# Load stage in program order, 33 early steps with a 128-column state, and two pieces of work moved ahead

## The chip, the cores and the metric

One core of one Trainium2 chip. The metric is device time in microseconds (us), the median of several runs; one more execution is taken by the hardware profiler. Engines: TensorE (PE; its weight loads are shown apart as PEld), VectorE (DVE), ScalarE (ACT), GpSimd (POOL) and SyncE (SP), which only issues DMAs here.

## The reference

Two layers on x of shape 16 x 128 x 64 x 64 (batch, channel, row, column), float32, each with a residual:

```python
x = x + _L0_conv_ref(_gn(x), ...)     # group norm, then a diagonal LSTM
x = x + _L1_conv_ref(_gn(x), ...)     # group norm, then a 4-qubit circuit per pixel
```

The diagonal LSTM skews the image (row i is shifted right by i, zeros are filled in) and scans over the columns of the skewed image:

```python
def step(carry, ist):
    h, c = carry
    h_shift = jnp.pad(h, ((0, 0), (0, 0), (1, 0)))[:, :, :-1]     # state of the row above
    s_s = einsum(w_ss[:, :, 0], h_shift) + einsum(w_ss[:, :, 1], h) + b_ss
    gates = ist + s_s                                             # ist: w_is @ x + b_is
    o, f, ig = split(sigmoid(gates[:, :3 * C])); g = tanh(gates[:, 3 * C:])
    c_new = f * c + ig * g
    h_new = o * tanh(c_new)
    return (h_new, c_new), h_new
```

A row that has not begun (its columns are still the filled zeros) also has a state. It depends neither on the image nor on the batch, only on how many steps have gone by: a chain of 64 vectors of 128 channels, the same for all waiting rows. The second layer projects 128 channels to four angles, needs sines of them, two matmuls with a square between, and adds the result.

## The kernel before

The 16 images stay in on-chip memory as a ring of 40 of the 64 rows (`ring`, L107); the other 24 pass through later. There are three stages.

**Load.** `rows(b)` (L361) loads 40 rows of image b into the ring in two DMAs of 1 MB and 256 KB on SP. The loop at L372 then loads the other 24 rows in three pieces of 256 KB (`rest`, a pool of 4 buffers), takes `bn_stats` of all eight pieces of 512 elements (L381) and `bn_aggr` (L382), always image by image: ring pieces first, then the rest pieces of the same image. These statistics give the first group norm; nothing of the scan can start without them: `group_mean` (L134), four VectorE operations, `group_rstd` (L140), then `normalised(0)` (L464) and `gate_ps(0)` (L485).

Beside that run the weights: eleven small DMAs on ACT's queue, twelve transposes in pairs of PSUM banks (L241 to L247), the circuit's coefficients on VectorE and ACT (L257 to L276), and the chain of waiting rows. `inv_step(j)` (L174) makes vector j+1 from vector j: four matmuls with the weights `wsT` and one moving column (L184), four activations (L194), three POOL products (L198 to L200), tanh (L202) and a scaling (L204), which gives `hinv[j+1]`, the input of the next. `EARLY` = 27 of them are spread over the images of the load. The load stage is ordered by the planner, not by hand.

**Scan.** 160 steps (`step`, L571), from L694 on in program order. At step t up to 32 row slots are active, in two bands; each step has the state products (L582), the gates' activations (L608), the cell update, and the input products of the next step (L491). A narrow step (`plain`, at most 96 columns) multiplies the state by w1T and w0T directly; a wide one takes wsT first and then differences. While fewer than 32 slots are active one waiting row advances with the step (`waits`, L548), from vector `EARLY` on. In steps 32 to 37 the last vectors are made by `inv_step` inside the step (L578 and the `next(inv, None)` lines), for L677 to read later. Four or six `bn_stats` of finished rows per step (`statistics`, L535) prepare the second group norm: group g is four rows of all 16 images, and group 9 of 16 ends with step 135.

**Join and quantum layer.** After the last step the statistics that are left (20 pieces), then over all 32 half-pieces of each image (L703 to L715): sum, group mean, deviations, squares, sum, `group_rstd`; then `w_image` (L721) and the images of the second layer, bound by DMA and TensorE in turn.

Queues are in program order per engine: a waiting instruction holds all behind it on its engine. DMAs on SP wait for a free buffer in the same way.

Of the kernel before, what the change touches and what calls it, by code (L numbers as in the profile page):

```python
# [11 lines left out]
F32 = mybir.dt.float32  # L12
# [15 lines left out]
EARLY = 27  # L28
# [50 lines left out]
def kernel(  # L79
# [60 lines left out]
    def group_rstd(pool, psum, var, rstd, which, scale):  # L140
        ps = psum.tile([P, NB], F32, name=f"gv{which}", tag="small")
        nc.tensor.matmul(ps, lhsT=group, rhs=var, start=True, stop=True)
        nc.vector.tensor_scalar(var, ps, scale, EPS, ALU.mult, ALU.add)
        sd = pool.tile([P, NB], F32, name=f"sd{which}", tag="gn_sd")
        nc.scalar.activation(sd, var, AF.Sqrt)
        r0 = pool.tile([P, NB], F32, name=f"r0{which}", tag="gn_r0")
        nc.vector.reciprocal(r0, sd)

        nc.vector.tensor_mul(sd, r0, r0)
        nc.vector.tensor_mul(sd, sd, var)  # L150
        nc.vector.tensor_scalar(sd, sd, -0.5, 1.5, ALU.mult, ALU.add)
        nc.vector.tensor_mul(rstd, r0, sd)  # L152

    small = ctx.enter_context(tc.tile_pool(name="small", bufs=2))
    with ExitStack() as scan:
# [13 lines left out]
        for v in (*hst, *xns, none):  # L169
            nc.gpsimd.memset(v, 0.0)  # L170
# [3 lines left out]
        def inv_step(j, pool=None):  # L174


            one = ps_small.tile([P, 4], F32, name=f"inv_ps{j}", tag="small") if pool is None else None
            ps = {}
            for g in ORDER:
                if pool is None:  # L180
                    ps[g] = one[:, g : g + 1]
                else:
                    ps[g] = pool.tile([P, 1], F32, name=f"inv_ps{j}_{g}", tag=f"inv{g}")
                nc.tensor.matmul(  # L184
                    ps[g],
                    lhsT=wsT[:, g * 128 : (g + 1) * 128],
                    rhs=hinv[:, j : j + 1],
                    start=True,
                    stop=True,
                )  # L190
            yield
            ac = small.tile([P, 4], F32, name=f"inv_a{j}", tag="inv_a")
            for g in ORDER:
                nc.scalar.activation(ac[:, g : g + 1], ps[g], FUNC[g], bias=bias[:, g : g + 1])  # L194
            yield
# [7 lines left out]
            yield  # L203
# [3 lines left out]

        with ExitStack() as prep:
            pp = prep.enter_context(tc.tile_pool(name="prep", bufs=1))
            rest_pool = prep.enter_context(tc.tile_pool(name="rest", bufs=4))  # L210
            ps_prep = prep.enter_context(tc.tile_pool(name="ps_prep", bufs=2, space=PSUM))
            ps_inv = prep.enter_context(tc.tile_pool(name="ps_inv", bufs=1, space=PSUM))


            wx_n = pp.tile([P, 4, P], F32, name="wx_n")
            ws_n = pp.tile([P, 4, 2 * P], F32, name="ws_n")
            nc.scalar.dma_start(out=wx_n, in_=w_is.rearrange("(g o) c -> o g c", o=P))
            nc.scalar.dma_start(out=ws_n, in_=w_ss.rearrange("(g o) c k -> o g (c k)", o=P))
            b_n = pp.tile([8, P], F32, name="b_n", tag="rows")
            nc.scalar.dma_start(out=b_n[0:4], in_=b_is.rearrange("(g o) -> g o", o=P))  # L220
            nc.scalar.dma_start(out=b_n[4:8], in_=b_ss.rearrange("(g o) -> g o", o=P))
            nc.scalar.dma_start(out=wide_sb, in_=wide)
            four_sb = pp.tile([4, 272], F32, name="four_sb")
            nc.scalar.dma_start(out=four_sb, in_=four)
            qw = pp.tile([P, 24], F32, name="qw")
# [3 lines left out]
            prew = pp.tile([4, P], F32, name="prew")  # L229
            preb = pp.tile([4, 1], F32, name="preb")  # L230
            post_n = pp.tile([P, 4], F32, name="post_n")
            nc.scalar.dma_start(out=prew, in_=pre_w)
            nc.scalar.dma_start(out=preb, in_=pre_b.rearrange("(w one) -> w one", one=1))
            nc.scalar.dma_start(out=post_n, in_=post_w)
            nc.scalar.dma_start(out=b_out, in_=post_b.rearrange("(o one) -> o one", one=1))

            ident = pp.tile([P, P], F32, name="ident")
            make_identity(nc, ident)


            for g in range(4):  # L241
                for n, (dst, src) in enumerate(
                    ((wxT, wx_n[:, g, :]), (w0T, ws_n[:, g, 0::2]), (w1T, ws_n[:, g, 1::2]))
                ):
                    tp = ps_prep.tile([P, P], F32, name=f"tp{g}_{n}", tag="tp")
                    nc.tensor.transpose(tp, src, ident)
                    nc.scalar.copy(dst[:, g * 128 : (g + 1) * 128], tp)  # L247
            nc.vector.tensor_add(wsT, w0T, w1T)
            tp = ps_prep.tile([P, 8], F32, name="bias_ps", tag="tp")
            nc.tensor.transpose(tp, b_n, ident[0:8, 0:8])  # L250
            nc.scalar.copy(bias, tp[:, 0:4])
            nc.vector.tensor_add(bias, bias, tp[:, 4:8])
            nc.vector.memset(hinv[:, 0:1], 0.0)
            nc.vector.memset(cinv[:, 0:1], 0.0)
# [4 lines left out]
            nc.vector.tensor_add(ang[:, 1, 0, :], q3[:, 0, :], q3[:, 2, :])  # L259
            nc.vector.tensor_sub(ang[:, 1, 1, :], q3[:, 0, :], q3[:, 2, :])  # L260
            nc.vector.tensor_copy(ang[:, 1, 2, :], q3[:, 1, :])
            nc.vector.tensor_scalar(
                ang[:, 0], ang[:, 1], 1.0 / (4.0 * math.pi), 0.25, ALU.mult, ALU.add
            )
            nc.vector.tensor_scalar_mul(ang[:, 1], ang[:, 1], 1.0 / (4.0 * math.pi))
            rnd = pp.tile([P, 2, 3, 8], F32, name="rnd")
            nc.vector.tensor_scalar(rnd, ang, ROUND, ROUND, ALU.add, ALU.subtract)
            nc.vector.tensor_sub(ang, ang, rnd)
            trig = pp.tile([P, 2, 3, 8], F32, name="trig")
            nc.scalar.activation(trig, ang, AF.Sin, scale=TWO_PI)  # L270
            co = gates.tile([P, 8, 8], F32, name="co")
            nc.vector.tensor_mul(co[:, 0], trig[:, 0, 0, :], trig[:, 0, 2, :])
            nc.vector.tensor_mul(co[:, 1], trig[:, 1, 0, :], trig[:, 0, 2, :])
            nc.vector.tensor_mul(co[:, 2], trig[:, 0, 1, :], trig[:, 1, 2, :])
            nc.vector.tensor_mul(co[:, 3], trig[:, 1, 1, :], trig[:, 1, 2, :])
            nc.vector.tensor_scalar_mul(co[:, 4:8], co[:, 0:4], -1.0)  # L276


            tp = ps_prep.tile([P, 16], F32, name="wt_ps", tag="tp")
            nc.tensor.matmul(tp, lhsT=prew, rhs=four_sb[:, 0:16], start=True, stop=True)  # L280
            nc.gpsimd.memset(w_image, 0.0)
            for j in range(8):
                nc.scalar.copy(w_theta[:, 16 * j : 16 * j + 16], tp)
            tp = ps_prep.tile([P, 1], F32, name="bt_ps", tag="tp")
            nc.tensor.matmul(tp, lhsT=four_sb[:, 16:144], rhs=preb, start=True, stop=True)
# [605 lines left out]
```

## Time and profile before

| | |
|---|---|
| median of 3 runs | 1467.23 us (1466.18 to 1468.28) |
| profiled execution, its time | 1469.78 us |
| its span | 1468.0 us |
| mean granted TensorE clock | 0.984 |
| busy: PE, PEld, DVE, ACT, POOL | 1363.1, 968.9, 975.8, 767.7, 889.9 us |
| HBM read, written | 59.61 MB, 46.14 MB |
| load: first TensorE product of the scan starts at | 110.73 us |
| scan: last statistics of the last step begin at | 1298.87 us |
| quantum layer: first angles at | 1314.52 us |

The span runs from the first to the last instruction; the execution's own time has some 2 us around it. Busy times of TensorE are of pipelined instructions and their ends are modelled, so a busy TensorE need not be one at its peak. A float32 product shows as two instructions. Idle time of an engine costs nothing where the engine isn't the one waited for.

### The profile page before, as it was taken

The numbers are of one execution on the slowest core, as the hardware profiler recorded it, in microseconds if no ns is written. First come the engines' busy times: TensorE is split into PE (matmuls) and PEld (weight loads), VectorE is DVE, ScalarE is ACT, GpSimd is POOL, SyncE is SP. The second block draws the span as 40 slices with busy tenths as digits, with TensorE's granted clock in tenths as the row PEclk, the third lists the DMA queues.
The fourth block names the chain that finished last, engine by engine and source line by source line (L and its number), as shares of the span: only waits on it lengthen the run. The fifth ranks groups of instructions, "written<-read, shape, count | busy, mean of one in ns | idle before, by whom it ended". The sixth has DMA issues, their size and how long they took to land. (4 is left out here: it accounts for less than half of the span.)

```text
span 1468.0 us, 19391 instructions
## 1 busy us (share of the span) xinstructions
PE 1363.1 (93%) x5798; PEld 968.9 (66%) x5798; DVE 975.8 (66%) x2458; ACT 767.7 (52%) x1862; POOL 889.9 (61%) x1694
## 2 busy tenths in 40 slices
PE   4658999999999999999999999999999999858987
PEld 3648887777776677667766776677677787842322
DVE  6883566566666666887777675555555687767775
ACT  3544666565555555555555555555555565533231
POOL 1115777766776677778887776677667676521110
PEclk9999999999999999999999999999999999979996
DMA  9980000000000000133344000000000000028996
GB/s 306 359 277 1 1 2 0 1 1 1 1 0 1 1 0 1 58 115 116 127 138 137 2 1 0 1 1 1 1 1 1 1 1 2 1 86 288 316 333 236
DMA packets 86192, 106.99 MB, mean 73 GB/s; under 512 B 4024, under 2 KB 70728, under 8 KB 86088
## 3 DMA queue, kind: packets, MB, share of 16 engines
q1 hardware_dynamic: 80576, 92.29, 18.6%
q0 software_dynamic: 3840, 12.59, 2.5%
q10 hardware_dynamic: 1672, 0.89, 0.2%
q8 instruction: 46, 0.75, 0.2%
q14 instruction: 58, 0.48, 0.1%
HBM read 59.61 MB, written 46.14 MB: 72 GB/s over the span
## 5 line engine op out<-in xcount | busy, mean ns | idle before, releaser
L491 PE MATMUL ps<-xn,wxT 128*128 128x512 f32 (+18 forms) x1280 | 480.7, 518 | 2.0 <-POOL xn L483 2.0
L604 DVE TENSOR_TENSOR ps<-ps,both 128x256 f32<-128x256 f32 (+9 forms) x544 | 219.7, 408 | 325.6 <-PE ps L582 320.0
L608 ACT ACTIVATE ps<-ps,bias 128x512 f32<-128x512 f32 (+23 forms) x480 | 268.4, 581 | 253.0 <-DVE ps L604 213.1
L491 PEld LDWEIGHTS ps<-xn,wxT 128*128 128x128 f32 x1280 | 231.8, 191 | 174.5 <-issue 155.5
L633 ACT COPY both<-ps 128x256 f32<-128x256 f32 (+9 forms) x544 | 191.5, 355 | 178.6 <-PE ps L582 158.9
L582 PE MATMUL ps<-diff,w1T 128*128 128x256 f32 (+14 forms) x1088 | 283.7, 363 | 0.0
L582 PE MATMUL ps<-diff,w0T 128*128 128x256 f32 (+14 forms) x1088 | 283.2, 362 | 0.0
L524 POOL TENSOR_TENSOR ring<-ring,hst 128x256 f32<-128x256 f32 (+8 forms) x488 | 247.2, 538 | 24.7 <-DVE hst L672 24.7
L582 PEld LDWEIGHTS ps<-hst,wsT 128*128 128x128 f32 x1088 | 195.9, 190 | 85.5 <-DVE hst L672 35.4
L582 PE MATMUL ps<-hst,wsT 128*128 128x256 f32 (+14 forms) x1088 | 241.3, 365 | 5.7 <-DVE hst L672 4.2
L582 PEld LDWEIGHTS ps<-diff,w0T 128*128 128x128 f32 x1088 | 199.7, 190 | 21.2
L582 PEld LDWEIGHTS ps<-diff,w1T 128*128 128x128 f32 x1088 | 199.2, 190 | 20.9
L483 POOL TENSOR_TENSOR xn<-xn,rstd 128x512 f32<-128x512 f32 (+10 forms) x160 | 170.7, 1067 | 15.2 <-DVE rstd L152 2.7
L478 POOL TENSOR_TENSOR xn<-ring 128x256 f32<-128x256 f32 (+8 forms) x213 | 147.1, 700 | 0.0
L672 DVE TENSOR_TENSOR hst<-g,ps 128x256 f32<-128x256 f32 (+13 forms) x320 | 108.5, 369 | 45.0 <-ACT g L663 41.7
L663 ACT ACTIVATE g<-cst 128x256 f32<-128x256 f32 (+20 forms) x320 | 103.0, 368 | 63.8 <-DVE cst L662 63.3
L473 POOL TENSOR_TENSOR xn<-ring,mean 128x16 f32<-128x16 f32 (+8 forms) x247 | 130.5, 537 | 7.0 <-DVE mean L138 6.0
L515 POOL TENSOR_TENSOR diff<-hst 128x240 f32<-128x240 f32 (+9 forms) x136 | 103.2, 759 | 39.0 <-DVE hst L672 35.6
L662 DVE TENSOR_TENSOR cst<-cst,ps 128x256 f32<-128x256 f32 (+20 forms) x320 | 104.6, 368 | 5.5
L659 DVE TENSOR_TENSOR ps<-ps,g 128x512 f32<-128x512 f32 (+20 forms) x160 | 95.2, 595 | 19.1 <-ACT g L608 17.8
L685 POOL COPY edge<-hst 128x16 f32<-128x16 f32 x64 | 25.1, 392 | 136.0 <-DVE hst L672 136.0
L652 DVE TENSOR_TENSOR cst<-cst,ps 128x512 f32<-128x512 f32 (+20 forms) x160 | 92.8, 580 | 16.9 <-ACT ps L608 9.4
(152 smaller groups left out, 1217.6 us busy)
## 6 DMA issues: line engine op xcount, KB each, us to landing
ring<-in_x_dram SPq DMA_DIRECT2D x16, 1024.0 KB, 7.6
out_dram<-ring SPq DMA_DIRECT2D x16, 1024.0 KB, 5.7
rest<-in_x_dram SPq DMA_DIRECT2D x48, 256.0 KB, 5.2
low<-ring SPq DMA_DIRECT2D x6, 2048.0 KB, 7.5
ring<-in_x_dram SPq DMA_DIRECT2D x6, 2048.0 KB, 8.1
low<-low POOLq DMA_DIRECT2D x48, 256.0 KB, 5.2
out_dram<-low SPq DMA_DIRECT2D x48, 256.0 KB, 5.1
ring<-in_x_dram SPq DMA_DIRECT2D x16, 256.0 KB, 7.9
```

Source lines behind the costliest of these rows:

```text
L473: nc.gpsimd.tensor_sub(by_pairs(xn, 0, j, n), x0, over(mean1, n))
L478: nc.gpsimd.tensor_sub(by_pairs(xn, 1, j, n), lower, of)
L483: nc.gpsimd.tensor_mul(v, v, r)
L491: nc.tensor.matmul(ps[g][:, :, a:b], lhsT=wxT[:, g * 128 : (g + 1) * 128], rhs=xns[t % 2][:, :, a:b], start=True, stop=True,)
L515: nc.gpsimd.tensor_sub(diff[:, 0, a1:b], now[:, 1, a1 - NB : b - NB], now[:, 0, a1:b])
L524: nc.gpsimd.tensor_add(x1, x1, by_pairs(new, q, j, n))
L582: nc.tensor.matmul(out, lhsT=w[:, g * 128 : (g + 1) * 128], rhs=rhs, start=False, stop=True, skip_group_check=True,)
L604: nc.vector.tensor_add(v, v, both[g][:, a:b])
L608: nc.scalar.activation(to[:, :, a:w], ps[g][:, :, a:w], FUNC[g], bias=bias[:, g : g + 1])
L633: nc.scalar.copy(both[g][:, a:b], ps[g][:, 0, a:b])
L662: nc.vector.tensor_add(c[:, q], c[:, q], ig[:, q])
L672: nc.vector.tensor_mul(new[:, q, a:v], th[:, q, a:v], act[GO][:, q, a:v])
```

## The change

Load stage: it is put into program order by hand. SP's order becomes `rows(b+2)`, then the rest pieces of image b+1 (`behind`); VectorE takes the ring pieces of image b+1 before the rest pieces of image b. `rest` has 7 buffers, four of which hold weights at first. The first image comes in five pieces. Six of the small loads go from ACT's queue to POOL's, `w_ss` comes first and its two taps are added before the transposes; four transposes share one PSUM bank and one copy. The circuit's coefficients are made on POOL. The other weights' transposes stand between the first five waiting-row steps.

Waiting rows: 33 steps in place of 27 are made in the load and none in the scan. The moving operand is the state vector read 128 times (a broadcast), and each step is followed by two matmuls whose result nobody reads (`keep`).

Hand-over: the state products of step 0 are issued before the statistics' last part; the input products add to them. Three more `keep` products stand before the first group mean and one after the variance's matmul.

Second statistics: once group 9 is done (`FIRST` = 10 groups), `early_sums` makes their mean, deviations, squares and sums, one operation per scan step, ahead of that step's `statistics`. At the end only six groups are left, taken about that mean, and one matmul turns both sums into group values. `inverse_root` has one operation fewer than `group_rstd`.

```diff
-EARLY = 27
+EARLY = 33
+FIRST = 10
...
-    def group_rstd(pool, psum, var, rstd, which, scale):
-        ps = psum.tile([P, NB], F32, name=f"gv{which}", tag="small")
-        nc.tensor.matmul(ps, lhsT=group, rhs=var, start=True, stop=True)
-        nc.vector.tensor_scalar(var, ps, scale, EPS, ALU.mult, ALU.add)
...
+    def inverse_root(pool, var, rstd, which):
+
         r0 = pool.tile([P, NB], F32, name=f"r0{which}", tag="gn_r0")
...
+        nc.scalar.activation(sq, var, AF.Sqrt)
+        nc.vector.reciprocal(r0, sq)
+        nc.vector.tensor_mul(sq, r0, r0)
+        nc.vector.scalar_tensor_tensor(sq, sq, -0.5, var, ALU.mult, ALU.mult)
+        nc.vector.scalar_tensor_tensor(rstd, sq, 1.5, r0, ALU.add, ALU.mult)
...
+        def inv_step(j, pool):
+
+
             ps = {}
+            rhs = hinv[:, j : j + 1].to_broadcast([P, P])
             for g in ORDER:
...
+                ps[g] = pool.tile([P, P], F32, name=f"inv_ps{j}_{g}", tag=f"inv{g}")
+                w = wsT[:, g * 128 : (g + 1) * 128]
+                nc.tensor.matmul(ps[g], lhsT=w, rhs=rhs, start=True, stop=True)
...
-            rest_pool = prep.enter_context(tc.tile_pool(name="rest", bufs=4))
...
+            rest_pool = prep.enter_context(tc.tile_pool(name="rest", bufs=7))
...
+            prep.enter_context(tc.manual_schedule())
+
+            ws_n = [rest_pool.tile([P, 2, 2 * P], F32, name=f"ws_n{i}", tag="rest") for i in range(2)]
+            sum_n = rest_pool.tile([P, 4, P], F32, name="sum_n", tag="rest")
+            wx_n = rest_pool.tile([P, 4, P], F32, name="wx_n", tag="rest")
...
+            def keep(pool, tag, v):
+
+                ps = pool.tile([P, v.shape[-1]], F32, name=nc.get_next_instruction_name(), tag=tag)
+                nc.tensor.matmul(ps, lhsT=ident, rhs=v, start=True, stop=True)
 
             rows(0)
             rows(1)
+            behind(0)
+            turned()
+            for k in (1, 2):
+                statistics(0, k)
...
+            transposed("wsT", wsT, lambda g: sum_n[:, g, :])
+            biases()
+            coefficients()
...
             for b in range(NB):
                 if b + 2 < NB:
                     rows(b + 2)
...
+                if b + 1 < NB:
+                    behind(b + 1)
+                    for k in (1, 2, 3, 4, 0):
+                        statistics(b + 1, k)
+                for k in (5, 6, 7):
+                    statistics(b, k)
+                aggregated(b)
                 while b < NB - 1 and done * (NB - 1) < EARLY * (b + 1):
-                    for _ in inv_step(done, ps_inv):
-                        pass
+                    inv_step(done, ps_inv)
+                    keep(ps_keep, "keep", ring[:, 2, b, 0:P])
+                    keep(ps_keep, "keep", wsT[:, 0:P])
+                    if between:
+                        between.pop(0)()
                     done += 1
...
+            first = {}
+            for g in ORDER:
+                first[g] = ps_gate.tile([P, 2, NC], F32, name=f"ps0_{g}", tag="gate")
+                for w, rhs in ((w1T, hst[0][:, :, 0 : LEAST // 2]), (w0T, above(hst[0], 0, LEAST // 2))):
+                    nc.tensor.matmul(
...
+            for v in (ring[:, 2, NB - 1, :], rests[NB - 1][0], rests[NB - 1][1]):
+                keep(ps_small, "small", v)
+
             group_mean(ps_small, mv1[:, :, 0], mean1, 1, 1.0)
...
+            nc.tensor.matmul(ps, lhsT=group, rhs=var, start=True, stop=True)
+            keep(ps_gate, "gate", wxT)
+            nc.vector.tensor_scalar_add(var, ps, EPS)
+            inverse_root(pp, var, rstd1, 1)
...
+        def early_sums():
+            k = 2 * FIRST
+            total(moments[:, 0], 0, k)
+            yield
+            group_mean(ps_small, moments[:, 0], mean2, 2, 1.0 / k)
+            less_mean(0, k)
+            yield
+            total(moments[:, 0], 0, k)
+            yield
+            yield from squared(0, k)
+            total(moments[:, 1], 0, k)
...
-        j = t + EARLY - 2
-        inv = inv_step(j) if SLOTS <= t and j < NH - 1 else iter(())
...
+            for later in sums:
+                next(later, None)
             statistics(4 if w - a <= LEAST else 6)
...
+            k, n = 2 * FIRST, 2 * NG2
+            less_mean(k, n)
+            total(more[:, 0], k, n)
+            for _ in squared(k, n):
+                pass
+            total(more[:, 1], k, n)
+            nc.vector.tensor_add(moments, moments, more)
+            ps = ps_small.tile([P, 2, NB], F32, name="gm3", tag="small")
+            nc.tensor.matmul(ps, lhsT=group, rhs=moments, start=True, stop=True)
+            nc.vector.tensor_scalar_mul(moments, ps, 1.0 / n)
+            var = small.tile([P, NB], F32, name="var2", tag="gn_var")
+            nc.vector.tensor_mul(var, moments[:, 0], moments[:, 0])
+            nc.vector.tensor_sub(var, moments[:, 1], var)
+            nc.vector.tensor_scalar_add(var, var, EPS)
+            inverse_root(small, var, rstd2, 2)
+            nc.vector.tensor_add(mean2, mean2, moments[:, 0])
```

## The prediction

> **What bounds the kernel now.** I read the page's slices first, then busy time by stretches of a few us, then the timeline of each stretch that the diff touches, and the chain of waits at the end.
>
> ```profile
> PE   4658999999999999999999999999999999858987
> DMA  9980000000000000133344000000000000028996
> ```
>
> Each digit is 36.7 us. There are three stages: the load (to 106 us, DMA near full, TensorE half idle), the scan (TensorE full to 1299 us), and the quantum layer. The diff touches the load, the hand-over to the scan, six scan steps, a few late steps and the join at 1299 to 1313 us.
>
> In the load, by stretches (busy us of PE, PEld, DVE, ACT, POOL, then granted clock, DMA share, GB/s):
>
> ```profile
> 40.00:50.00 10.00, 6.47 (x28) 6.21 (x29) 8.56 (x16) 5.24 (x21) 1.72 (x9) 1.00 1.07 372
> ...
> 96.00:98.00 2.00, 1.29 (x7) 1.21 (x6) 1.45 (x3) 1.27 (x6) 0.58 (x3) 1.00 0.45 161
> 98.00:100.00 2.00, 1.68 (x8) 1.68 (x8) 1.52 (x3) 0.99 (x4) 0.19 (x1) 1.00 0.47 145
> ```
>
> DMA bounds the middle (the five rows from 40 to 90 us average 365 GB/s). It falls below half at the end, where SP's last loads of `rest` wait for statistics to free one of four buffers, and also at 22 to 28 us (173 to 255 GB/s).
>
> **Part 1, load order.** The load moves 34.5 MB from 2.5 us on. At 365 GB/s the last byte lands at 2.5 + 94.5 = 97.0 us; I add 0.7 for a start in smaller pieces: 97.7. Before, the last piece was read at 105.4. But VectorE now ends later than one piece behind: when the 1 MB of image 15 lands, 1.75 MiB (5.0 us) are still to come, while 11 statistics of 0.60 us and two aggregations of 0.35 are still to do: 7.3 us, so it ends 2.3 us after the last byte, at 100.0, where before it ended at 106.5. **Gain 6.5.** Best case: no start loss and 372 GB/s, ends 97.6, gain 8.9. Worst: images 1's three `rest` pieces take over the buffers of the weights, which are only freed by the transposes put between the waiting rows' steps (about 21 us), and SP holds image 3 behind them. 5.4 MB are issued ahead of that wait and last to 17.4 us, so 5 us of DMA would be lost, less the 0.7 counted: gain 2.2. Six small weight loads move from ACT's queue to POOL's: a POOL issue costs 6.78/12 = 0.57 us here (at 1299.67), 3.4 us in all; POOL had nothing to do from 4 to 23 us. Some 14 small VectorE operations and the memsets go to POOL and delay its first waiting-row product to about 15 us; counted below in the start of that chain.
>
> **Part 2, 33 steps beside the load.** One step now, from the timeline (start, duration, engine, line, operation; in brackets the idle time before it and what ended it):
>
> ```profile
> 28.88 1.86 PE L184 MATMUL inv_ps<-hinv,wsT 128*128 128x1 f32 x8 [1.03 <-ACT hinv L204]
> ...
> 30.36 0.26 ACT L194 ACTIVATE inv_a<-inv_ps,bias 128x1 f32<-128x1 f32 x1 [0.17 <-PE inv_ps L184]
> ...
> 31.77 1.87 PE L184 MATMUL inv_ps<-hinv,wsT 128*128 128x1 f32 x8 [1.03 <-ACT hinv L204]
> ```
>
> It lasts 2.89 us: 1.48 until the third gate's activation (first gate 0.62, then twice 0.43, the pace of TensorE), and 1.41 through ACT, POOL and ACT. TensorE runs at half rate here although the granted clock reads 1.00: eight one-column matmuls take 1.87, and the same weights in the scan take 0.95. The new state has 128 columns and two filler matmuls per step. Were TensorE at full rate, the first gate would be there after 0.53 (four 128-wide instructions in the scan took 0.75 at 117.11, less two of 0.11), the others 0.22 apart: 0.97 + 1.41 = **2.38 us**. At half rate the wider drain adds 0.16 (my middle between 0.11, one pass, and 0.25 from the cold step at 112.39): **3.05 us**. Start: the first 256 KB of weights landed at 6.7 us, now it is `w_ss` in two such pieces (about 7.5), then two VectorE adds, four transposes (1.7) and a copy: `wsT` about 11 us; the table load of 1.28 and POOL behind its memsets (2.7 us for the six) put the first step at 13.5; five steps with transposes between them at 3.1, then 28 at 2.38: the chain ends at 95.7, under the load's 100.0, with 4.3 us of cover. It costs nothing; cover gone is the third rival.
>
> Which rate? [...]
>
> ```profile
> 1444.00:1446.00 2.00, 1.44 (x5) 0.80 (x6) 2.00 (x4) 0.42 (x1) 0.00 (x0) 1.00 0.10 34
> 1446.00:1448.00 2.00, 2.00 (x5) 0.37 (x3) 2.00 (x4) 0.00 (x0) 0.00 (x0) 0.71 0.32 111
> ```
>
> Here the clock falls with gaps of no more than 1 us, after groups of eight `po` matmuls (1.14 us when dense) every 3 us, a duty near 40%. The new step at full rate has 12 instructions of 0.11: 1.3/2.38 = 55%; at half rate 2.64/3.05 = 87%, which would raise the clock again, as 3 us of dense matmuls did at 1354.7. By the row, then, a mix, about 2.65. The quantum layer's images at some 75% duty (1.85 + 1.98 + 2.2 us of matmuls in 8) stay at 1.00. 55% lies between; I take 2.38, for the half rate does not sustain itself, and keep 2.65 and 3.05 for the rivals.
>
> **Part 3, hand-over.**
>
> ```profile
> 110.73 2.07 PE L491 MATMUL ps<-xn,wxT 128*128 128x128 f32 x8 [2.03 <-POOL xn L483]
> ...
> 113.69 0.27 ACT L608 ACTIVATE ps<-ps,bias 128x40 f32<-128x40 f32 x1 [3.23 <-PE ps L582]
> ...
> 117.11 0.49 PE L582 MATMUL ps<-hst,w1T 128*128 128x128 f32 x2 [0.21 <-DVE hst L505]
> ```
>
> Step 0 is 6.38 us from its input products to the next step; 16 state products stand between, at half rate. They now run before the statistics end. Left are the input products (third gate at 0.53 + 0.5 = 1.03) and the 1.66 us from there to the new state (115.45 to 117.11): 2.7, **gain 3.7** at full rate. At half rate third gate 1.73, and step 1 is slower by 1.6: gain about 1.2. The fillers leave up to 2 us of idle TensorE before it, so I take 3.0. The statistics chain loses one 0.21 operation and, at full rate, some 0.15 at each of two matmuls: **0.5**.
>
> **Part 4, six steps out of the scan.** L184 leaves steps 32 to 37:
>
> ```profile
> 283.64 1.89 PE L582 MATMUL ps<-hst,wsT 128*128 128x256 f32 x8
> 292.25 1.89 PE L582 MATMUL ps<-hst,wsT 128*128 128x256 f32 x8
> 293.98 0.95 PE L184 MATMUL inv_ps<-hinv,wsT 128*128 128x1 f32 x8
> 301.76 1.89 PE L582 MATMUL ps<-hst,wsT 128*128 128x256 f32 x8
> ```
>
> A step is 9.51 us with them, 8.61 without, TensorE never idle: 6 x 0.90 = **gain 5.4**, the surest part.
>
> **Part 5, second statistics ahead.** At the end, 1305.53 to 1312.99, five operations over 512 elements (0.86 each) and a matmul in between:
>
> ```profile
> 1305.53 0.84 DVE total L706
> ...
> 1311.61 0.23 ACT sd L145
> ...
> 1312.99 0.43 DVE w_image L721
> ```
>
> That is 7.46 us. New: five over 192 elements at 0.44 (between 0.86 for 512 and 0.21 for 16) 2.2, add 0.22, matmul 0.69, four small 0.84, root 0.25, reciprocal 0.29, four small 0.84: 5.33. **Gain 2.1.** The moved part isn't free. Group 9's statistics end in step 139, so the early sums fall on steps 140 to 145, each ahead of that step's statistics in VectorE's queue.
>
> ```profile
> 1219.10 2.05 DVE L539 BATCH_NORM_STATS2 stats<-ring 128x6 f32<-128x256 f32 x6
> ...
> 1221.07 0.93 DVE L604 TENSOR_TENSOR ps<-ps,both 128x160 f32<-128x160 f32 x3
> ...
> 1224.50 1.25 PE L582 MATMUL ps<-hst,wsT 128*128 128x144 f32 x8 [0.47 <-DVE hst L672]
> ```
>
> In step 141 VectorE is already late and TensorE waits for it. The mean's matmul stands behind the four half products (1219.8), VectorE waits for it to 1220.25, scales (0.2), subtracts over 320 elements (0.6), and only then starts the six statistics: they end 2.0 us later than now, and the gates' adds, hence the state, with them. Step 142 adds 0.6, step 143 0.3 (0.27 of VectorE idle), 140, 144 and 145 nothing (1.4 us idle and more). **Loss 2.9**, between 0.9 (VectorE gets its mean while it would wait anyway) and 3.5.
>
> The quantum layer is unchanged and starts earlier by the sum; its loads were there at 1307.
>
> **Sum.** -6.5 - 0.5 - 3.0 - 5.4 - 2.1 + 2.9 = -14.6. The span is 1468.0, its execution 1469.8, the runs' median 1467.2; the edits lie inside the span, so I take the sum from the median: **1452.6 us**.
>
> **Rivals.** (a) SP waits for the weights' buffers: gain 2.2 in place of 6.5: 1456.9. For it: 7 buffers, four held by weights at first, and SP's order. Against: a buffer of image 0 may come free first. (b) The clock swings, 2.65 a step: the chain ends 13.5 + 15.5 + 74.2 = 103.2; copies 0.5, state products 2.5 and three fillers 3.0 stand ahead of the mean's matmul on TensorE: 109.2 against 106.6 before, +2.6; step 0 -3.7, the rest -5.1: 1461. (c) **Slower:** half rate throughout, 3.05 a step: the chain ends at 114.2, and with 0.5, 3.5 and 4.3 ahead of it the mean's matmul starts at 122.5, +15.9; less 8.8: about 1474. It decides from the step's length: the chain is late from 2.5 us on, and at about 2.85, near today's 2.89, the whole gain is gone. For it: today's half rate. Against: 87% duty. (d) VectorE hides the early sums and the DMA runs at its best: 1448.
>
> **How the numbers follow.** Forecast with its own spread, 1449 to 1455: 0.55; (a) 0.18; (b) 0.12; (c) 0.05; (d) 0.10. The range 1446 to 1461 leaves out (c) and the ends of (b) and (d). A change within 0.2% (2.9 us) is about what cannot be told from none. Faster 0.93, same 0.03, slower 0.04: (c) with a part of (b).
>
> **What would show it.** 33 groups of eight L184-like matmuls at 2.4 us each; the last at 96 us; no L184 in the scan and steps 32 to 37 at 8.6; DMA above 340 GB/s to 97; step 0 under 3.4 us; step 141 longer by 2. Wrong if the waiting rows' chain ends after the statistics, or SP stands still near 20 us.

## The result, and the profile after

The changed kernel takes **1455.72 us** (median of 7 runs, 1454.82 to 1459.08); the kernel before, run beside it on the same chip, 1466.18 us (7 runs, 1460.93 to 1468.28). The ratio is 0.9939, 95% interval 0.9922 to 0.9956: 10.5 us less, where 14.6 had been forecast. The profiled execution took 1455.38 us, with a span of 1453.4. The two profiled spans differ by 14.6 us, the forecast's own number, but that is luck: 4.2 us of it lie in the unchanged quantum layer (153.5 us before, 149.3 after).

The same two slices as before, 36.3 us to a digit: the load, the scan and the quantum layer are as they were, and TensorE is busier in the load.

```profile
PE   6778999999999999999999999999999999858987
DMA  9970000000000000144433000000000000027997
```

The load by stretches (busy us of PE, PEld, DVE, ACT, POOL, then granted clock, DMA share, GB/s):

```profile
60.00:90.00 30.00, 22.77 (x147) 18.00 (x145) 26.76 (x47) 18.07 (x77) 7.48 (x39) 1.00 1.08 363
90.00:98.00 8.00, 5.30 (x34) 4.17 (x34) 7.18 (x13) 2.84 (x8) 1.01 (x6) 1.00 1.07 366
98.00:100.00 2.00, 0.46 (x1) 0.40 (x2) 2.00 (x4) 0.00 (x0) 0.00 (x0) 0.91 0.41 152
100.00:102.00 2.00, 1.94 (x3) 0.46 (x2) 1.97 (x5) 0.00 (x0) 0.00 (x0) 0.50 0.01 2
```

DMA is full to 98 us. After that its share falls off over two us:

```profile
98.00:98.50 0.50, 0.00 (x0) 0.00 (x0) 0.50 (x2) 0.00 (x0) 0.00 (x0) 1.00 0.68 250
98.50:99.00 0.50, 0.00 (x0) 0.00 (x0) 0.50 (x2) 0.00 (x0) 0.00 (x0) 1.00 0.44 164
99.00:99.50 0.50, 0.00 (x0) 0.00 (x0) 0.50 (x2) 0.00 (x0) 0.00 (x0) 1.00 0.33 123
99.50:100.00 0.50, 0.46 (x1) 0.40 (x2) 0.50 (x2) 0.00 (x0) 0.00 (x0) 0.64 0.19 70
```

The 16 DMA engines did not end together. Had they done so, the last byte would have come at about 98.8 (0.41 of two us); the last transfer was issued at 94.5 and landed 6.1 us later, at 100.6. VectorE is busy without a pause from 96.04 to 103.42 us. The timeline (start, us, engine, line, operation, in brackets the idle time before it and what ended it) has the chain of waiting rows first, then the end of the load, the hand-over, steps 32 to 37, the early sums and the join:

```profile
28.02 1.16 PE L177 MATMUL inv_ps<-hinv,wsT 128*128 128x128 f32 x8 [0.46 <-ACT hinv L188]
30.41 1.16 PE L177 MATMUL inv_ps<-hinv,wsT 128*128 128x128 f32 x8 [0.46 <-ACT hinv L188]
...
96.04 3.06 DVE L263 BATCH_NORM_STATS2 stats<-ring 128x6 f32<-128x512 f32 x5 [0.53 <-DMA ring<-in_x_dram]
99.02 1.86 DVE L263 BATCH_NORM_STATS2 stats<-rest 128x6 f32<-128x512 f32 x3
...
103.05 0.37 DVE L266 BATCH_NORM_AGGREGATE mv<-stats 128x2 f32<-128x48 f32 x1
103.52 0.37 PE L138 MATMUL gm<-mv,wide_sb 128*128 128x16 f32 x2
107.00 3.41 PE L565 MATMUL ps<-xn,wxT 128*128 128x128 f32 x16 [0.87 <-POOL xn L556]
110.47 0.49 PE L694 MATMUL ps<-hst,w1T 128*128 128x128 f32 x2
...
285.88 1.89 PE L694 MATMUL ps<-hst,wsT 128*128 128x256 f32 x8
294.49 1.89 PE L694 MATMUL ps<-hst,wsT 128*128 128x256 f32 x8
...
1208.82 0.75 DVE L628 TENSOR_TENSOR stats<-stats,mean 128x320 f32<-128x320 f32 x1
1209.46 2.03 DVE L651 BATCH_NORM_STATS2 stats<-ring 128x6 f32<-128x256 f32 x6
...
1214.85 1.40 PE L694 MATMUL ps<-hst,wsT 128*128 128x144 f32 x8 [1.19 <-DVE hst L776]
...
1297.38 0.42 DVE L628 TENSOR_TENSOR stats<-stats,mean 128x192 f32<-128x192 f32 x1
...
1302.59 0.42 DVE L823 TENSOR_TENSOR w_image<-w_theta,rstd 128x256 f32<-128x256 f32 x1
```

Where the time went, read from such lines of both profiles. The last column is a second execution of the same changed kernel, taken later as an experiment.

| stretch | forecast | first profile | second profile |
|---|---|---|---|
| mean's matmul, before at 106.58 | -6.5 | 103.49: -3.1 | 106.32: -0.3 |
| from there to the first input product, before 4.15 | -0.5 | 3.51: -0.6 | 3.49: -0.7 |
| from there to step 1, before 6.38 | -3.0 | 3.47: -2.9 | 3.51: -2.9 |
| steps 32 to 37 | -5.4 | -5.4 | -5.4 |
| steps 141 to 145 with the early sums | +2.9 | +3.7 | +3.0 |
| last statistics to `w_image`, before 14.12 | -2.1 | 11.87: -2.25 | 11.88: -2.24 |
| **first angles, before at 1314.52** | **-14.6** | 1304.12: -10.4 | 1306.30: -8.2 |

From the mean's matmul to the first angles the kernel before took 1207.9 us, the changed one 1200.6 and 1200.0: 7.3 and 7.9 us gained where the forecast has 8.1. What is missing is missing in one stretch, the load.

The quantum layer, which no edit touches, took between 148.9 and 153.5 us in the fourteen profiled executions of all kernels here. So the experiments are read by two marks of the profile, the mean's matmul and the first angles, and the medians stand beside them.

### The profile page after: what moved, and what is told of

Same layout as the page of the kernel before. It is cut to its first block, busy times and chain, and to the rows that moved or that the text cites. A ratio compares the mean times of both kernels' runs of the same rounds, so it can differ in the third digit from the quotient of the medians.

```text
span 1453.4 us, 19718 instructions
## 1 busy us (share of the span) xinstructions
PE 1371.0 (94%) x5942; PEld 966.9 (67%) x5942; DVE 976.8 (67%) x2450; ACT 766.1 (53%) x1855; POOL 897.6 (62%) x1717
## 5 line engine op out<-in xcount | busy, mean ns | idle before, releaser
L546 POOL TENSOR_TENSOR xn<-ring,mean 128x16 f32<-128x16 f32 (+8 forms) x247 | 130.6, 538 | 11.4 <-DVE mean L139 10.4
L713 ACT ACTIVATE g<-ps,bias 128x512 f32<-128x512 f32 (+20 forms) x160 | 97.3, 608 | 11.5 <-PE ps L694 3.5
```

Source lines behind the costliest of these rows:

```text
L546: nc.gpsimd.tensor_sub(by_pairs(xn, 0, j, n), x0, over(mean1, n))
L713: nc.scalar.activation(to[:, :, a:w], ps[g][:, :, a:w], FUNC[g], bias=bias[:, g : g + 1])
```

## The experiments

Medians of the kernel before, run beside them: 1465.18 us for e1 to e4, 1466.06 for e5 to e8, 1465.14 for e9 to e12.

### e5 to e8: what the 128 copies and the fillers are worth

```diff
# e5: this and the next edit; e7: this one alone
-            rhs = hinv[:, j : j + 1].to_broadcast([P, P])
+            rhs = hinv[:, j : j + 1]
...
# e6: this one alone
-                    keep(ps_keep, "keep", ring[:, 2, b, 0:P])
-                    keep(ps_keep, "keep", wsT[:, 0:P])
...
# e8: the kernel before, with nothing but this
-EARLY = 27
+EARLY = 33
```

> The changed kernel, but the waiting rows' steps have one moving column again and no filler matmuls beside them. My theory: TensorE stays at half rate, a step takes 2.9 in place of 2.39 us, the chain of 33 ends at about 108 to 109 in place of 93.4 us, after the statistics (103), and with the state products and fillers behind it, at half rate, the mean's matmul starts at 112 to 116: the whole kernel is 9 to 12 us slower than the changed one and about as long as before. Rival (the transposes between the first steps have raised the clock, and the chain holds it): steps of 2.4 us and no difference.

> The changed kernel without the two filler matmuls per waiting-row step; the 128 columns stay. At full rate TensorE would have eight instructions of 0.11 us in 2.39 us, a duty of 37%. My theory (a duty near 40% lets the clock fall, as at 1446 us of the kernel before): it swings or stays at half rate, steps average 2.6 to 3.05 us and the chain ends at 100 to 114 us. Rival [...]: steps stay at 2.39 and nothing changes.

> The changed kernel with one moving column in the waiting rows' steps, and the two filler matmuls of 128 columns kept: they alone stream columns, four instructions of 0.11 us in 2.4 us, a duty of 18%. My theory: the clock falls, steps of 2.9 us, the chain ends at about 108 us, as without fillers. Rival [...]: steps of 2.3 to 2.4 us.

> The kernel before with EARLY = 33 and nothing else: 33 waiting-row steps at half rate in its load stage, none in the scan. My theory: the chain starts at 22 us and takes 2.89 us a step, so it ends at 22 + 33 x 2.9 = 118 us; the scan's first state products wait for it, while the statistics' end (106.6) and the first input product (110.7) stay, so step 1 starts about 7 to 8 us later than at 117.1; steps 32 to 37 give back 5.4: 1 to 3 us slower than before. Rival (the chain has slack): 5.4 us faster.

| | one column | 128 columns |
|---|---|---|
| no fillers | e5: 1468.62 us, ratio 1.0019 (1.0001 to 1.0038), step 2.90 us, mean at 117.1 | e6: 1473.72, 1.0042 (1.0023 to 1.0061), step 3.11, mean at 121.1 |
| two fillers a step | e7: 1475.06, 1.0068 (1.0050 to 1.0086), step 2.99, mean at 123.4 | changed kernel: 1455.72, 0.9939, step 2.39, mean at 103.5 |

Neither part gains by itself: with only one of them, and all the rest of the change, the kernel is slower than before; with both it is faster. One step of e5, with a stretch of the load:

```profile
51.59 1.86 PE L177 MATMUL inv_ps<-hinv,wsT 128*128 128x1 f32 x8 [1.03 <-ACT hinv L188]
```

```profile
60.00:90.00 30.00, 19.42 (x84) 18.57 (x84) 26.86 (x47) 15.80 (x62) 5.77 (x30) 1.00 1.08 362
```

In e6 TensorE did come to full rate, and lost it again:

```profile
18.94 1.28 PE L177 MATMUL inv_ps<-hinv,wsT 128*128 128x128 f32 x8 [0.18 <-ACT hinv L188]
21.45 1.16 PE L177 MATMUL inv_ps<-hinv,wsT 128*128 128x128 f32 x8 [0.76 <-ACT hinv L188]
23.85 1.16 PE L177 MATMUL inv_ps<-hinv,wsT 128*128 128x128 f32 x8 [0.70 <-ACT hinv L188]
...
30.21 2.08 PE L177 MATMUL inv_ps<-hinv,wsT 128*128 128x128 f32 x8 [1.03 <-ACT hinv L188]
```

```profile
24.00:26.00 2.00, 1.12 (x9) 0.82 (x9) 1.41 (x4) 1.61 (x13) 0.58 (x3) 1.00 1.08 363
26.00:28.00 2.00, 1.61 (x6) 1.39 (x7) 2.00 (x4) 0.66 (x4) 0.00 (x0) 0.51 1.07 374
...
60.00:90.00 30.00, 19.68 (x77) 16.78 (x76) 26.29 (x46) 14.75 (x58) 5.61 (x29) 0.50 1.08 362
```

The three steps at 2.4 us fall while weights are still being transposed in the pauses; without those a step has 8 instructions of 0.11 us in 2.4, a duty (the share of a step that its instructions take at full rate) of 37%, and from 26 us on the granted clock is 0.50 until the chain is over. With the fillers it is 12 in 2.39, 55%, and 1.00. The longest pause in those three steps is 1.3 us. A pause alone did not decide it here. In the changed kernel's quantum layer TensorE waited 2.63 us for a DMA, in a stretch where it was busy 5.37 of 8 us, and stayed at full rate (0.62 us for two such products; in the kernel before, at 1434.04 us, they took 1.06 at a granted clock of 0.50):

```profile
1338.00:1346.00 8.00, 5.37 (x32) 1.25 (x34) 5.12 (x8) 1.82 (x3) 1.36 (x3) 1.00 1.04 382
1344.03 0.62 PE L864 MATMUL theta<-low,w_image 128*32 128x512 f32 x2 [2.63 <-DMA low<-low]
```

That the duty decides is my reading of these runs, 37% with the clock lost and 55% with it held; no run varies the duty while the pauses stay the same.

e8 gives the price of the cheap way, 33 steps in the old form: they end after the statistics, whose last aggregation is at 104.0, and the mean's matmul stands behind them on TensorE.

```profile
115.64 1.86 PE L184 MATMUL inv_ps<-hinv,wsT 128*128 128x1 f32 x8 [1.03 <-ACT hinv L204]
117.37 0.59 PE L137 MATMUL gm<-mv,wide_sb 128*128 128x16 f32 x2
```

1473.34 us, ratio 1.0049 (1.0037 to 1.0062): moving the six steps costs more than it gains unless the step is made shorter too.

### e1 and e2: the sums taken ahead

```diff
# e1: all sums at the join, as before the change
-                if (g, i) == (FIRST - 1, NB - 1):
-                    sums.append(early_sums())
...
-            k, n = 2 * FIRST, 2 * NG2
-            less_mean(k, n)
+            n = 2 * NG2
+            total(moments[:, 0], 0, n)
+            group_mean(ps_small, moments[:, 0], mean2, 2, 1.0 / n)
+            less_mean(0, n)
...
# e2: ahead, but two groups later
-FIRST = 10
+FIRST = 12
```

> The changed kernel without the early sums: all 32 half-pieces per image are summed after the last step. My theory: steps 141 to 146 lose the 3.7 us that they gained in length (step 141 back from 7.8 to 5.9 us), and the join from the last statistics of the last step to w_image grows from 11.9 to about 13.9 us (one operation fewer than before's 14.1), so the first angles start 1.6 us earlier than the changed kernel's 1304.1, at about 1302.5. Rival (the steps are longer for another reason, such as the throttle): the steps keep their length, and the angles start 2.0 us later, at about 1306.

> The changed kernel with FIRST = 12: the early sums begin when group 12's statistics are done, and so fall on the narrow steps from 148 on, where VectorE idles some 0.6 us per step between the cell product and the gates' product. My theory: what the early sums cost is set by the step they fall on; steps 141 to 146 lose the 3.7 us, the narrow steps gain 0.1 to 0.3 us each for six steps plus some 0.7 for the mean's matmul, 1.5 to 2 in all, and the join is 0.6 shorter (128 in place of 192 elements in five operations): first angles at 1301.3 to 1302.3. Rival (the cost is that of the operations wherever they stand): 3.7 us again, angles near 1303.5.

e1: median 1457.01 us, ratio 0.9954 (0.9937 to 0.9971). With the mean's matmul at 103.53, as in the changed kernel, the first angles came at 1302.69, **1.43 us earlier**. The step lengths say why: from step 140 on e1 has 5.81, 5.86, 5.80, 5.44, 5.11 us, the changed kernel 5.80, 7.76, 6.95, 5.86, 5.11. The sums cost 3.6 in the scan, and the join without them is 13.9 us instead of 11.9.

But the 6.95 of step 142 is an accident of that one execution. TensorE ran at half rate there, with a granted clock of 0.50 from 1216 to 1218 us. The first two lines are of the first profile, the third is the same work in e12:

```profile
1216.00:1218.00 2.00, 2.00 (x11) 2.00 (x10) 2.00 (x7) 0.44 (x2) 2.00 (x5) 0.50 0.00 0
1216.04 1.17 PE L694 MATMUL ps<-diff,w1T 128*128 128x144 f32 x4
...
1218.75 0.65 PE L694 MATMUL ps<-diff,w1T 128*128 128x144 f32 x4
```

In the seven other profiles with the sums in these steps (e3 to e7, e9, e12) step 142 takes 6.3 us, and the sums cost 3.0. From the mean's matmul to the first angles e12 needs 1200.0 us and e1 1199.2. So taken ahead the sums lose some 0.8 us more than they save. The medians don't show it.

e2: median 1457.87, 0.9949 (0.9927 to 0.9970). Its load ended late (mean at 106.28), so from there: 1199.9 us to the first angles, against 1200.6 in the changed kernel's first profile, 1200.0 in its second, 1199.2 in e1. That is no clear gain over ten groups: the narrower steps do not hide the sums either (they cost 2.9 us there).

### e4: more fillers in the hand-over

```diff
-            for v in (ring[:, 2, NB - 1, :], rests[NB - 1][0], rests[NB - 1][1]):
+            for v in (ring[:, 2, NB - 1, :], *[wxT] * 7):
...
-            keep(ps_gate, "gate", wxT)
+            for _ in range(2):
+                keep(ps_gate, "gate", wxT)
```

> The changed kernel with other filler matmuls at the hand-over: seven 512-column products of weights that are there already in place of the two that wait for the last image's pieces, and two in place of one after the variance. My theory: TensorE no longer idles from 95.9 to 99.5 us, the clock stays full, and step 0 (first input product to step 1's first product) takes 2.7 in place of 3.47 us: 0.8 us gained. Rival (the fillers hold up the mean's matmul, in order on TensorE): it starts later than VectorE's last aggregation by up to 1 us and nothing is gained.

Median 1459.24, ratio 0.9963 (0.9954 to 0.9972). The granted clock stayed at 1.00 from 90 to 110 us, the sixteen input products took 2.05 us instead of 3.41, and step 1 followed them by 2.96 instead of 3.47: the clock is worth **0.5 us** there. But the statistics ended at 104.7 and the mean's matmul had to let the fillers pass:

```profile
104.32 0.37 DVE L266 BATCH_NORM_AGGREGATE mv<-stats 128x2 f32<-128x48 f32 x1
...
105.72 1.13 PE L332 MATMUL I-1401_1402<-wxT,ident 128*128 128x512 f32 x2
106.91 0.39 PE L138 MATMUL gm<-mv,wide_sb 128*128 128x16 f32 x2
```

2.2 us lost for 0.5 gained: seven were too many.

### e3: the ring in five transfers for every image

```diff
-            pieces = [(1, 5), (0, 1)]
+            pieces = [(1, 2), (2, 3), (3, 4), (4, 5), (0, 1)]
```

> The changed kernel with every image's ring rows in five DMAs of 256 KB, as image 0 has them, in place of 1 MB and 256 KB. My theory: VectorE ends 4 us after the last byte because it can't begin an image's ring pieces before the whole 1 MB has landed; with single pieces it loses no 0.55 us per image, runs ahead, and the mean's matmul starts at 100.5 to 101.5 in place of 103.5 us: 2 to 3 us gained. Rival 1 (VectorE is at its throughput by itself): 103.5 stays, or 0.5 us earlier. Rival 2 (eight DMAs per image in place of five are limited by how many may be in flight): the DMA falls below 360 GB/s and the matmul starts later than 103.5.

Median 1457.00, ratio 0.9948 (0.9932 to 0.9965), mean's matmul at 103.90, so no gain. The two halves of that are in the trace. The tail became shorter: from the landing of the last image's first rest piece (which starts a filler) to the mean's matmul 2.56 us, against 3.98 in the changed kernel.

```profile
101.34 1.10 PE L332 MATMUL I-1428_1429<-rest,ident 128*128 128x512 f32 x2 [2.48 <-DMA rest<-in_x_dram]
...
103.90 0.36 PE L138 MATMUL gm<-mv,wide_sb 128*128 128x16 f32 x2 [0.28 <-PE I-1431_1432 L332]
```

But that landing was 1.8 us later: from 8 to 12 and from 12 to 20 us the load ran at 265 and 322 GB/s (323 and 362 in the changed kernel). In the first 30 us SP stood 7.6 us until earlier transfers of its own to the ring or to `rest` had landed (2.8 in the changed kernel), as e3's second rival has it.

### e12 and e9: why the load ends at different times

Of the profiles with the changed kernel's load order, the first and e1 have the last image's ring read from 96.04 us on, e4 from 97.30 and e2 from 98.62. e12 is the changed kernel once more. e9 has the weights' transposes ahead of the chain:

```diff
             biases()
+            transposed("w0T", w0T, lambda g: ws_n[g // 2][:, g % 2, 0::2])
+            transposed("w1T", w1T, lambda g: ws_n[g // 2][:, g % 2, 1::2])
...
-                lambda: transposed("w0T", w0T, lambda g: ws_n[g // 2][:, g % 2, 0::2]),
-                lambda: transposed("w1T", w1T, lambda g: ws_n[g // 2][:, g % 2, 1::2]),
```

> The changed kernel itself once more, for comparison on the same chip and for the spread between executions. Theory: median 1455.7, mean's matmul between 103.5 and 106.3 according to when TensorE comes to full rate in the chain's first steps: if w1T's transposes run at 22.8 us rather than 19.7, SP waits over 1 us for them. Rival (the profiled execution of the changed kernel is typical and the load ends at the same time in each): mean's matmul at 103.5 within 0.3.

> The changed kernel with the transposes of w0T and w1T taken out of the chain's pauses and put ahead of the 33 steps, right behind wsT and the biases. Theory (SP's last rest transfer of image 2 waits for w1T's transposes, which release the buffer of the weights; they ran at 19.7 us in the changed kernel's profile but at 22.8 us where TensorE came to full rate later, and the load then ended up to 2.7 us later): SP no longer waits for w1T, no row below 350 GB/s between 20 and 28 us, mean's matmul at 102.5 to 103.9 in whatever execution, first angles at 1303.2 to 1304.6; median 1.0 us below the changed kernel's of this call. Rival (the load's end spreads because the queue's first 16 us do): mean's matmul still anywhere from 103.5 to 106.3, no difference of the medians.

e12: median 1456.85 us (6 runs), ratio 0.9949 (0.9934 to 0.9963). Its mean's matmul is at 106.32, 2.8 us after that of the first profile of the same kernel. Timeline, SP's waits (total, times, longest) and stretches of e12:

```profile
16.56 2.08 PE L177 MATMUL inv_ps<-hinv,wsT 128*128 128x128 f32 x8 [1.00 <-ACT hinv L188]
...
22.50 0.64 PE L301 MATMUL w1T_ps<-ident,ws_n 128*128 128x128 f32 x4
...
98.83 3.07 DVE L263 BATCH_NORM_STATS2 stats<-ring 128x6 f32<-128x512 f32 x5 [0.52 <-DMA ring<-in_x_dram]
```

```profile
SPq L239 <- PE w1T_ps L301: 1.0, 1, 1.0
```

```profile
20.00:22.00 2.00, 2.00 (x14) 1.92 (x12) 1.50 (x4) 1.19 (x5) 0.19 (x1) 1.00 0.94 271
26.00:28.00 2.00, 1.49 (x11) 1.00 (x10) 1.60 (x4) 1.61 (x10) 0.58 (x3) 1.00 0.91 291
```

In the first profile TensorE was at full rate from the chain's second step (1.16 us at 15.51), `w1T` was transposed at 19.66, and no stretch between 20 and 28 us is below 348 GB/s. Here the second step ran at half rate (2.08), `w1T` came at 22.50, SP's last rest piece of image 2 waited for the buffer that it releases, and the load ran at 319 GB/s from 20 to 28 us. e2 and e4 are alike (SP waits 1.2 and 1.4 us for `w1T`, 310 and 312 GB/s). e1 is the exception that limits this reading: it waited 2.3 us, dipped to 354 only, and ended its load like the first profile.

The dip is only a part of the 2.8 us: 319 in place of 365 GB/s over 8 us are 1.0 us of load. The traces hold the rest. The landing of image 15's 1 MB is recorded in 16 parts, and VectorE went on with the last: in the first profile that part came at 96.01 us and VectorE started at 96.04.

| image 15's 1 MB | first part | last part | apart |
|---|---|---|---|
| changed kernel, first profile | 93.39 | 96.01 | 2.6 |
| e1 | 93.75 | 96.02 | 2.3 |
| e4 | 94.34 | 97.28 | 2.9 |
| e2 | 94.75 | 98.59 | 3.8 |
| e12 | 94.48 | 98.81 | 4.3 |
| e9 | 93.72 | 95.73 | 2.0 |

The executions that waited and dipped (e4, e2, e12) have their first part 1.0 to 1.4 us later than the first profile. The other 1.7 us of e12 lie in the distance between the parts, which differs from one execution to the next, also of the same kernel. In e12 it rises from 2.6 to 4.3 us near 35 us and stays. What sets it is not shown.

e9: no wait for `w1T` beyond 0.2 us, 365 GB/s from 20 to 28 us, mean's matmul at 103.24, first angles at 1303.22, as the theory had them. e10 and e11 below, with the same edit, have 364 and 364. The median, 1456.54 (ratio 0.9945, 0.9931 to 0.9958), is only 0.3 below e12's and doesn't confirm the gain of 1.0 that was expected: with 6 runs each, spread over 3 us and more, it can't be told from none.

### e10 and e11: the parts that helped, together

```diff
# e10: e9's edit, e1's edit, and the last three images' rings in five transfers
-            for k0, k1 in (...) if b == 0 else pieces:
+            for k0, k1 in (...) if b == 0 or b > NB - 4 else pieces:
...
# e11: e10, and
-            for v in (ring[:, 2, NB - 1, :], rests[NB - 1][0], rests[NB - 1][1]):
+            for v in (ring[:, 2, NB - 1, :], wxT, wxT, rests[NB - 1][0], rests[NB - 1][1]):
...
             keep(ps_gate, "gate", wxT)
+            keep(ps_gate, "gate", wxT[:, 0:256])
```

> The changed kernel with three edits: w0T and w1T ahead of the chain, the ring pieces of the last three images in five transfers instead of two, and no sums of the second statistics ahead (all of them at the join, as before the change). Theory: VectorE no longer idles 0.55 us ahead of each of the last images' rings, so mean's matmul comes 2.6 us instead of 4.0 us after the last image's first rest piece has landed, at 102.1; the step lengths 141 to 146 are those of the kernel before and the join is longer (together 1.4 us gained, as the run without early sums had it); first angles at 1301.3, median 1452.9, which is 2.8 us below the changed kernel's of this call. Rival (VectorE's operations, not its pauses, set the end, and five waits cost what they save): mean's matmul at 103.5, first angles at 1302.7.

> The kernel of e10_combined with three more filler products: two on wxT ahead of the two on the last image's rest pieces (they fill TensorE's pause from 96.7 to 99.5 us) and one half-width on wxT behind the variance's matmul. Theory (a pause of 2.8 us lowers the clock just ahead of the input products): granted clock 0.9 or more from 98 to 110 us, sixteen input products in 2.1 us instead of 3.4, step 1 begins 0.5 us sooner after the gates' first product, first angles at 1300.8. Rival (the fillers stand in the way of the mean's matmul, or the clock falls for other reasons): mean's matmul later by 0.5 us or more, no gain.

e10: mean's matmul at 102.18, 2.58 us after the landing; first angles at 1301.25, both as forecast. The median, 1456.45 (ratio 0.9941, 0.9926 to 0.9956), is 3.5 us above the 1452.9 that was expected with these marks: its runs spread from 1453.63 to 1458.24. Within every kernel here the longer runs are those with the lower mean granted clock (correlations of -0.57 to -0.98). e10's six have a median of 0.9805, e11's 0.987. In both profiles the clock averages 1.00 from 110 to 1290 us and 0.73 to 1.00 by stretches of 40 us behind it, so the lapses are in the quantum layer; what brings them on is not shown.

e11: median **1452.96 us** (1450.81 to 1456.20), ratio 0.9922 (0.9906 to 0.9939), the fastest of all kernels here: 3.9 us below the changed kernel run beside it (e12), though the two intervals still overlap. Its profile:

```profile
99.03 1.10 PE L332 MATMUL I-1398_1399<-rest,ident 128*128 128x512 f32 x2 [0.78 <-DMA rest<-in_x_dram]
...
101.58 0.37 PE L138 MATMUL gm<-mv,wide_sb 128*128 128x16 f32 x2 [0.27 <-PE I-1401_1402 L332]
...
104.92 1.06 PE L332 MATMUL I-1416_1417<-wxT,ident 128*128 128x256 f32 x2
105.78 2.31 PE L566 MATMUL ps<-xn,wxT 128*128 128x128 f32 x16
```

The clock was 1.00 to 102 us but still fell to 0.50 at 104, so the theory of its fillers failed in the main; the extra one behind the variance then ran at half rate and held the input products for 0.7 us more than in e10, though they then took 2.31 us instead of 3.40. First angles at 1301.08, 0.17 before e10's. The difference between the medians of e10 and e11 is therefore not explained by the fillers.

## Why the prediction was right or wrong

**Load order (6.5 forecast, 3.1 and 0.3 measured): the step that failed.** The forecast has image 15's 1 MB landing at 97.7 - 5.0 = 92.7 us and 7.3 us of VectorE's work behind it. The work took 7.4 (96.04 to 103.42). The landing came at 96.0, 3.3 us late, and nearly all that is missing in the first profile is missing there. No run changes the load order alone; that it sets the mark, and not the chain of waiting rows, is read from VectorE, whose last aggregation ends just ahead of the mean's matmul.

- The rate is the smaller part. The first 8 us went as forecast (220 GB/s on average, 1.8 MB). From 8 to 12 us the load ran at 323 GB/s and from 30 to 90 us at 359 to 364, not 365. With all engines ending together that makes 98.8 us for the last byte, 1.1 us late.
- The larger part is that I had counted with a mean rate, as if the 16 DMA engines were one and each transfer ended before the next began. VectorE went on when the last part of the 1 MB had landed, and its parts came 2.6 us apart. When that last part was in (96.01), the first parts of the next three transfers had been in since 94.1, 94.8 and 95.5. The last transfer of all landed at 100.6 and not at 97.7. VectorE, which idled 0.55 us ahead of each image's ring, got its last large piece too late. e3, e10 and e11 show that the size of that piece matters: with smaller transfers the tail is 2.6 us instead of 4.0.
- Rival (a), SP behind the buffers of the weights, was priced at a gain of 2.2 and 1456.9 us. It is seen in part of the executions (e12, e2, e4), where it goes with 1.0 to 1.4 us, and is absent in the first profile. That the medians, 1455.72 and 1456.85, lie nearer to that rival's number than to the forecast's is therefore in good part luck: most of what is missing has the other cause. e9 takes the wait away and has the early end. What the forecast missed is that the wait depended on the second step's rate: `w1T` is in the chain's pauses, so TensorE at half rate delayed a DMA (by 1.0 us in e12). TensorE came to full rate before 15.51 us in the first profile and only at about 20.7 us in e12. Why two executions of one kernel differ by some 5 us there is not shown.

**33 steps beside the load (2.38 us a step, at no cost): right.** 2.39 measured. The first began at 10.3 instead of 13.5, the last ended at 93.4 instead of 95.7. Of the reason given, that 87% busy at half rate would raise the clock, the changed kernel shows the outcome: it rose from half rate in both profiles. As a rule it doesn't hold: e7 was busy 29.42 of 30 us and stayed at half rate. Rivals (b) and (c) were real alternatives, and both were one edit away: e6 is the clock lost until the chain ends (mean's matmul at 121.1, ratio above 1), e5 and e8 are half rate (117.1 and 117.3). (c) had been put at 122.5 and 1474 us; e7, a chain at half rate with fillers in the way, though of one column, has 123.4 and 1475.06. The row from 1444 to 1448 us was a good guide. There the clock fell with gaps of no more than 1 us and a duty near 40%; e6 idled no longer than 1.3 us in the steps ahead of the fall and lost the clock at 37%. That 55% would do was an estimate of mine. It held, but between 37 and 55% nothing here says where the edge is.

**Hand-over (3.0): right**, 2.9 twice. The clock had fallen to 0.50 as suspected, and e4 shows what full rate would have added: 0.5, so 3.4; the 3.7 of the working were 0.3 too many. **Statistics chain (0.5): right**, 0.6. **Six steps (5.4): right**, 5.4.

**Second statistics (a net loss of 0.8): right.** The join gained 2.25 (2.1). The sums cost 3.0 (2.9) in seven profiles of eight. Step 141 was 7.76 - 5.93 = 1.8 longer (2.0), step 142 6.3 - 5.8 = 0.5 (0.6). The first profile's 3.7, outside the 0.9 to 3.5, has the 0.65 us of half rate in step 142. So this part should not have been in the change: its own forecast was a loss, and e1, without it, has the earlier angles.

## What to carry to other kernels

The serial chain on TensorE was paced by the clock here (2.39 us a step at full rate, 2.90 to 3.11 at half), and the clock went with the duty (lost at 37%, held at 55%) and not with the longest pause (lost after 1.3 us, held over 2.63): count the busy time of one period before building the chain, and try wide operands and fillers together, since each alone made this kernel slower than it was. Plan a load by the landing of each transfer's last part, not by the mean rate: parts 2 to 4 us apart moved the end by as much. Where the last large transfer of a load is followed by smaller ones, ask what the consumer still has to do when it lands and not how many bytes come behind it. Cut the transfers only at the end, where it shortened the tail by 1.4 us, and not at the start, where the rate fell from 323 to 265 GB/s. Work that releases a DMA's buffer is better kept out of the pauses of a chain whose pace can vary; it went with about 1 us of later load in three of five executions here.

## What the runs showed of the hardware

A granted clock of 1.00 in these records is no proof of full rate; the duration of a known matmul tells it. In e5 and e7 it reads 1.00 while eight one-column matmuls take 1.86 and 1.71 us, and e7's two-instruction filler on `wsT` takes 0.80, as in e12 at 96.99 us, where the clock reads 0.50; at full rate it takes 0.49. The first step of every chain here is at or near half rate under a reading of 1.00 too: its eight matmuls take 1.83 to 2.05 us, against 1.16 at full rate with 128 columns and 0.95 with one.

Being busy by the record did not by itself raise the clock: in e7 TensorE was busy 29.42 of 30 us from 60 to 90 us and stayed at half rate. All three chains with one column (e5, e7, e8) stayed there, at 2.90, 2.99 and 2.89 us a step. That a one-column instruction adds nothing to the duty, as the 18% in e7's expectation has it, is an estimate and was not measured by itself.

A statistic's cost differed with how its input came: 0.60 us each when five wait in a landed 1 MB (3.06 for five), 0.64 to 0.70 when each has a transfer of its own (3.22 to 3.48 for five in e3).
